# Four graph layers on one core: the search for other relations in the second stage instead of at the front, and a first stage without a branch

## The chip, the core and the metric

The kernel runs on one core of a Trainium2 chip. The metric is the device time of one execution in microseconds, lower is better. The kernel before takes 2770.98 us, the median of three runs (2770.6 to 2774.85). Of one more execution there is a profile.

## What is computed

128 graphs of 128 nodes with 128 features each pass through four layers; each is `x = x + layer(relu(layernorm(x)), adj)`. The adjacency `adj` is int32 and in this input holds only 0 and 1. Cut to what matters:

```python
# layer 0: relational graph layer, 8 relations
for r in range(1, 8):
    mask = (adj == r)
    agg += (mask / clip(mask.sum(2), 1e-6)) @ h @ rel_weights[r]
out = relu(layernorm(agg + h @ self_w.T + self_b) * gamma + beta)
# layer 1: attention from all pairs of nodes
D = abs(h[:, :, None, :] - h[:, None, :, :])
z = D @ W1.T + b1                        # 64 features per pair
z = batchnorm(z)                         # mean and variance over ALL pairs of ALL graphs
s = leaky(z) @ W2 + b2
A = softmax(where(adj > 0, s, -9e15))
y = leaky(batchnorm(A @ h @ Wg.T + bg))  # again over all graphs
out = concat(h, y) @ Wt.T + bt
# layers 2 and 3: graph attention with 4 heads and with 1 head, masked with adj > 0
```

Relations 2 to 7 matter in layer 0 alone. With an adjacency of 0 and 1 their sums are zero, and what remains of the sum over relations is relation 1.

## The kernel before

**Stages.** The batch norms cut the work into three stages. Line numbers are those of the kernel before.

- *First stage* (L265 to L781): layer 0 for groups of four graphs (32 groups, `chain`), and for each graph the differences of all pairs. Each graph has four *tiles* of differences, 512 in all. A tile goes through `difference` (L304: DVE, or POOL for tiles 1 and 3; L315), `absolute` (L362: ACT, not for tile 0, which is made with a maximum), `products` (L319: PE, L325 and L328, into PSUM `hp`), `evacuate` (L332: ACT, L339, PSUM to `z`) and `statistics` (L348: DVE). Two tiles of `z`, 1 MB, are stored to DRAM by SP (L346).
- *Second stage* (L830 to L1142): slots, one per graph. A slot takes two halves of `z` (loaded through a ring of ten buffers, L717), applies the batch norm (ACT, L908 and L912) and the leaky ReLU (DVE, L926), multiplies with W2 on PE (`ps`, L883) and turns the sums on PE (`pk`, L890). Every four slots the scores of a group go to DRAM and back (`rows`, L960 and L967), and a chain of attention steps follows, spread over later slots. `at(slot, place, work)` puts work at a place of a slot; "l" is after the scores of the slot before.
- *Third stage* (L1157 on): layers 2 and 3 in two versions, chosen with the flag `bounded` (L1099), that is, whether the attention scores are small enough to leave out the softmax's maximum. In this input the first version runs.

**Order of work.** The order inside the first stage is fixed when the program is built. `_ordered` (L118) takes steps with an engine, an estimated cost, the steps that they follow, and a rank; it walks through time and emits for each engine what could begin earliest. Each engine then runs its instructions in this order. The second stage is written out by slots. `with tc.manual_schedule()` keeps the order.

**Layer 0 in the front.** Relations other than 1 are treated apart:

- `part` (L573) loads all of `adj` in 16 parts of 512 KB as 128x1024 int32; `highest` (L577) takes the maximum of even parts on DVE (L583) and a sum of ReLU(adj - 1) of odd ones on ACT (L581); L587 to L597 make `flag` of these. All steps of group 0's layer 0 and a part of group 1's (the names in `FRONT`, L34) are ordered around this search in a first plan.
- `tc.If(flag)` (L653) runs the general sum over relations for all groups and writes it to DRAM as `AGG`; `cmp.Else()` (L700) writes the bias row `selfb` there for 31 groups (L702, 1792 and 6144 KB). This input takes the second way.
- A second plan (L779) holds the rest of the first stage. Each group from the second on loads its `agg` (L435) and adds it in `joined` (L492); group 0 adds `selfb` directly.

**The steps of a group that are named below**: `mask` (POOL, L452, adj == 1), `m8` (POOL, L530: adj > 0 as uint8, kept for all stages in `M8`), `deg` and `per` (DVE), `rs`, `rso`, `rsx` (POOL: reciprocal roots; `RS` is the last one), `hn` (ACT), `share` (POOL), `pt`, `pm`, `ph`, `po` (PE), `hT`, `maskT`, `hw` (ACT), `o` (DVE, L492), `on` and `end` (DVE), `h1` (ACT, L506), and in `features` `xp` (PE), `xe` (ACT), "again" (POOL, L410, a copy beside `xe` so that shifted reads wrap around), `pw` and `xw`.

**Users of `M8`**: `cap` in the second stage (POOL, L972: M8 * BIG + NEG12) and `off` in the third (POOL, L1202: M8 == 0).

Of the kernel before, what the change touches and what calls it, by code (L numbers as in the profile page):

```python
# [17 lines left out]
P = 128  # L18
G = 4
EPS = 1e-5  # L20
BIG = 3e38
# [11 lines left out]
AHEAD = 1  # L33
FRONT = {"load", "mask", "mv", "deg", "rs", "most", "per", "hn", "share", "pt", "hT", "pm", "maskT", "ph", "hw", "m8",  # L34
         "sd", "nb"}
PARTS, HELD = 16, 6
# [7 lines left out]
SEARCHED, BIAS = 5.5, 22.0  # L44
# [73 lines left out]
def _ordered(steps, limits, hop):  # L118
# [4 lines left out]
    free, done = dict.fromkeys(("SP", "Pool", "ACT", "DVE", "PE", "DMA"), 0.0), {}  # L123
# [16 lines left out]
    while len(plan) < len(steps):  # L140
# [17 lines left out]
        done[name] = start + cost + (0 if engine != "SP" else SEARCHED if name[0] == "part" else LANDING)  # L158
# [13 lines left out]
def tile_gnn_stack(ctx: ExitStack, tc: tile.TileContext, a: dict, out: bass.AP):  # L172
# [7 lines left out]
    early = ctx.enter_context(ExitStack())  # L180
    early_ring = ctx.enter_context(ExitStack())
    psum = early.enter_context(tc.tile_pool(name="psum", bufs=1, space=bass.MemoryType.PSUM))
    banks = {"sm": 2}
# [35 lines left out]
    slots = [dr.tile([G, P, ROW], F32, tag=f"rows{n}", name=f"rows{n}") for n in range(2)]  # L219
    M8 = [res.tile([P, G, P], U8, tag=f"m{g}", name=f"m{g}") for g in range(NG)]  # L220
# [42 lines left out]


    with tc.tile_pool(name="c0", bufs=1) as c0, tc.tile_pool(name="p0", bufs=2) as p0, ExitStack() as ctx0:  # L265

        both = c0.tile([P, 2, P], F32, name="both")
# [3 lines left out]
        sizes = (7, NG - 8)  # L271
        rest = [dr.tile([P, n, G, P], F32, tag=f"a{i}", name=f"a{i}") for i, n in enumerate(sizes)]
        AGG = [t[:, i, :, :] for t, n in zip(rest, sizes) for i in range(n)]
        AGG = [None] * AHEAD + AGG
        selfb = const.tile([P, G, P], F32, name="selfb")


        XP = [psum.tile([P, 4, P], F32, tag=f"xp{n}", name=f"xp{n}") for n in range(2)]
        gamma, beta = (t[:, 2, :] for t in XP)

        def shift(mv, rs):

            nb = small.tile([P, G], F32, name="lnnb")
            nc.gpsimd.tensor_tensor(nb, mv[:, :, 0], rs, OP.mult)
            nc.gpsimd.tensor_scalar(nb, nb, -1.0, None, op0=OP.mult)
            return nb
# [5 lines left out]
        H1 = {}  # L292
# [4 lines left out]
        steps = []  # L297

        def step(name, engine, cost, after, rank, work, takes=(), gives=()):
            steps.append((name, engine, cost, after, takes, gives, rank, work))  # L300

        XE, XW, diffs, linear, halves, stats = {}, {}, {}, {}, {}, {}

        def difference(i):  # L304

            b, t = divmod(i, NT)
            xe, k = XE[b // 2], b % 2
            on_pool = t in ON_POOL
            d = p0.tile([P, 2, KC, P], F32, tag=f"d{int(on_pool)}", name="d")
            x = xe[:, k, 0:P] if on_pool else XP[b // 2 % 2][:, k, :]  # L310
            ahead = xe[:, k, 1 + KC * t:]
            ahead = bass.AP(tensor=ahead.tensor, offset=ahead.offset,
                            ap=[list(ahead.ap[0]), [KH, 2], [1, KC], [1, P]])
            eng = nc.gpsimd if on_pool else nc.vector
            eng.tensor_tensor(d, ahead, x[:, None, None, :].to_broadcast([P, 2, KC, P]),  # L315
                              OP.max if t == BY_MAX else OP.subtract)
            diffs[i] = d.rearrange("p h k i -> p h (k i)")

        def products(i):  # L319
            d = diffs.pop(i)  # L320
            hp = linear[i] = big("hp").rearrange("p a b -> p (a b)")
            by_max = i % NT == BY_MAX
            for c in range(0, KC * P, 512):
                for hh in range(2):
                    nc.tensor.matmul(hp[64 * hh:64 * hh + 64, c:c + 512], w1T2 if by_max else w1T,  # L325
                                     d[:, hh, c:c + 512], start=True, stop=not by_max, skip_group_check=True)
                for hh in range(2 * by_max):
                    nc.tensor.matmul(hp[64 * hh:64 * hh + 64, c:c + 512], XW[i // NT // 2][:, i // NT % 2, :],  # L328
                                     both_t.rearrange("p h k i -> p h (k i)")[:, hh, c:c + 512],
                                     start=False, stop=True, skip_group_check=True)  # L330

        def evacuate(i):  # L332

            b, t = divmod(i, NT)
            if t % 2 == 0:
                halves[b, t // 2] = held_z()
            if t == 0 and b % G == 0:
                stats[b // G] = p0.tile([P, 2 * NT + 1, G, 6], F32, name="st")
            nc.scalar.copy(half_of(b, t), linear.pop(i))  # L339

        def half_of(b, t):
            return halves[b, t // 2][:, t % 2 * KC * P:(t % 2 + 1) * KC * P]

        def kept(b, half):
            to = HP[b][:, half * NT // 2:(half + 1) * NT // 2, :]
            nc.sync.dma_start(to.rearrange("p a b -> p (a b)"), halves[b, half])  # L346
# [1290 lines left out]
```

## Time and profile before

| what | value |
|---|---|
| median of 3 runs | 2770.98 us |
| profiled execution: time | 2768.47 us |
| profiled execution: span, first to last instruction | 2766.7 us |
| busy: PE, DVE, ACT, POOL | 2450.3, 2470.4, 2386.6, 1717.5 us |
| mean granted TensorE clock | 0.972 |
| DMA: moved, mean rate | 636.17 MB, 230 GB/s |
| flag made (DVE, L597) | 35.4 us |
| first difference (DVE, L315) | 43.0 us |
| first copy out of `hp` (ACT, L339) | 63.6 us |
| statistics of group 0 closed (L359) | 113.6 us |
| statistics of group 31 closed (L359) | 1520.8 us |
| first step of the third stage (POOL, L1202) | 2308.5 us |

All times inside the execution are counted from the start of the span. "Busy" is the time in which an engine works on an instruction; the idle time ahead of an instruction is put down to what released it, in brackets with an arrow. Releasers are inferred from semaphore events; "issue" is time in which an engine waited for nothing that the profile shows. A busy PE isn't PE at its peak, since its products are pipelined. "xN" is a number of like instructions. SP mainly issues DMAs.

### The profile page before, as it was taken

What the parts mean: (1) busy time and instruction counts of PE and PEld (TensorE: products, weight loads), DVE (VectorE), ACT (ScalarE), POOL (GpSimd) and SP (SyncE); (2) the same over time, 40 slices, a digit from 0 to 9 for tenths busy, and PEclk for the clock granted to TensorE, in tenths of its full rate; (3) what the DMA queues carried; (4) which work ended last, traced back from release to release, by engine and by line L of the source; (5) the groups of instructions that cost most, each with busy time, mean ns of one, the idle gap of its engine ahead of it and who ended that gap; (6) DMA issues with size and microseconds to landing.
All of it is one profiled execution on the core that took longest, in us unless ns stands there. A gap on an engine that the chain in (4) does not pass through costs nothing.

```text
span 2766.7 us, 42019 instructions
## 1 busy us (share of the span) xinstructions
PE 2450.3 (89%) x14521; PEld 1181.3 (43%) x14521; DVE 2470.4 (89%) x4712; ACT 2386.6 (86%) x2837; POOL 1717.5 (62%) x1629
## 2 busy tenths in 40 slices
PE   4899999999999999999998799988988887999886
PEld 2333333333333333333332344444444445777775
DVE  4999999999999999999999698888888887899986
ACT  4899999999999999999998787887878776898985
POOL 5899999999999999999987001100010115665642
PEclk7999999999999999999999899999999998999998
DMA  8455555555555555555543899999999971121110
GB/s 294 196 194 208 219 203 210 204 211 204 208 212 209 207 210 207 210 205 215 204 196 126 325 409 411 410 410 410 409 408 410 410 289 55 47 70 58 58 32 25
DMA packets 196203, 636.17 MB, mean 230 GB/s; under 512 B 32771, under 2 KB 100486, under 8 KB 132486
## 3 DMA queue, kind: packets, MB, share of 16 engines
q1 hardware_dynamic: 195536, 633.14, 59.9%
q8 instruction: 120, 1.97, 0.3%
q14 instruction: 109, 0.89, 0.1%
q10 hardware_dynamic: 438, 0.17, 0.0%
HBM read 329.10 MB, written 304.15 MB: 229 GB/s over the span
## 4 chain that ended last, share of the span: by engine, by line
ACT 34%; PE 22%; DVE 18%; issue 11%; DMA 10%; POOL 3%; SPq 0%; ACTq 0%; POOLq 0%; DVEq 0%
ACT d L363 12%; ACT z L339 11%; PE hp L325 6%; PE ps L883 5%; DMA rows<-sk 4%; DVE d L315 3%; DVE z L926 3%; DMA u<-rows 3%; DMA z<-hp 3%; PE hp L328 2%; ACT h L1241 2%; PE pk L890 2%; ACT hn L465 2%; ACT o L465 2%; ACT h L506 1%
## 5 line engine op out<-in xcount | busy, mean ns | idle before, releaser
L315 POOL TENSOR_TENSOR d<-xe 128x2048 f32<-128x2048 f32 x256 | 1074.2, 4202 | 59.7 <-PE hp L325 55.7
L325 PE MATMUL hp<-d,w1T 128*64 128x512 f32 x4096 | 998.6, 602 | 114.7 <-ACT z L339 99.1
L363 ACT ACTIVATE d<-d 128x2048 f32<-128x2048 f32 x384 | 734.7, 1935 | 14.7 <-POOL d L315 14.6
L315 DVE TENSOR_TENSOR d<-xe,xp 128x2048 f32<-128x2048 f32 x256 | 579.7, 2265 | 16.9 <-POOL xe L410 7.5
L325 PEld LDWEIGHTS hp<-d,w1T 128*64 128x64 f32 x4096 | 286.3, 137 | 635.6 <-issue 465.2
L339 ACT COPY z<-hp 128x1024 f32<-128x1024 f32 x512 | 516.3, 1028 | 44.6 <-PE hp L328 26.7
L974 POOL TENSOR_TENSOR x<-x,bt 128x512 f32<-128x512 f32 x32 | 48.5, 1517 | 674.1 <-DMA x<-x 544.4
L353 DVE BATCH_NORM_STATS2 st<-z 128x6 f32<-128x512 f32 x512 | 349.6, 683 | 53.7 <-ACT z L339 53.0
L354 DVE BATCH_NORM_STATS2 st<-z 128x6 f32<-128x512 f32 (+1 forms) x512 | 329.5, 643 | 0.0
L926 DVE SCALAR_TENSOR_TENSOR z<-z 128x2048 f32<-128x2048 f32 x128 | 293.2, 2291 | 4.0 <-ACT z L908 3.9
L908 ACT ACTIVATE z<-z,bias,scale 128x2048 f32<-128x2048 f32 x128 | 267.2, 2087 | 9.6 <-DVE bias L821 7.9
L912 ACT ACTIVATE zr<-z,bias,scale 128x2048 f32<-128x2048 f32 x128 | 267.3, 2088 | 0.9 <-PE ps L883 0.5
L328 PE MATMUL hp<-both_t,xw 128*64 128x512 f32 x1024 | 267.5, 594 | 0.0
L883 PE MATMUL ps<-z,w2z 128*32 128x512 f32 x1024 | 141.4, 624 | 61.9 <-DVE z L926 61.7
L890 PEld LDWEIGHTS pk<-pick,su 128*128 128x128 f32 x1024 | 127.8, 196 | 136.4 <-DVE su L904 98.8
L890 PE MATMUL pk<-pick,su 128*128 128x16 f32 x1024 | 140.2, 269 | 23.2 <-DVE su L904 22.6
L1357 PE MATMUL pv<-wr,e 128*128 128x128 f32 x1024 | 139.3, 281 | 5.9 <-DVE e L1334 4.0
L883 PE MATMUL ps<-zr,w2r 128*32 128x512 f32 x1024 | 142.5, 629 | 0.0
L328 PEld LDWEIGHTS hp<-both_t,xw 128*64 128x64 f32 x1024 | 80.7, 137 | 139.9 <-issue 139.9
L883 PE MATMUL ps<-z,w2l 128*32 128x512 f32 x1024 | 139.2, 612 | 0.0
L1357 PEld LDWEIGHTS pv<-wr,e 128*128 128x128 f32 x1024 | 126.7, 194 | 13.3 <-DVE e L1334 4.1
L1334 DVE SCALAR_TENSOR_TENSOR e<-e,ps 128x512 f32<-128x512 f32 x160 | 106.9, 677 | 26.2 <-ACT ps L1331 25.6
(243 smaller groups left out, 3823.1 us busy)
## 6 DMA issues: line engine op xcount, KB each, us to landing
hp<-z SPq DMA_DIRECT2D x248, 1024.0 KB, 4.1
z<-hp SPq DMA_DIRECT2D x248, 1024.0 KB, 14.2
x<-x SPq DMA_DIRECT2D x118, 256.0 KB, 6.0
u<-rows SPq DMA_DIRECT2D x32, 384.0 KB, 11.6
x<-in_x_dram SPq DMA_DIRECT2D x32, 256.0 KB, 5.6
adj<-in_adj_dram SPq DMA_DIRECT2D x32, 256.0 KB, 5.8
part<-in_adj_dram SPq DMA_DIRECT2D x16, 512.0 KB, 6.6
out_dram<-x SPq DMA_DIRECT2D x32, 256.0 KB, 2.4
```

What stands on the lines that cost most here:

```text
L315: eng.tensor_tensor(d, ahead, x[:, None, None, :].to_broadcast([P, 2, KC, P]), OP.max if t == BY_MAX else OP.subtract)
L325: nc.tensor.matmul(hp[64 * hh:64 * hh + 64, c:c + 512], w1T2 if by_max else w1T, d[:, hh, c:c + 512], start=True, stop=not by_max, skip_gr ...
L328: nc.tensor.matmul(hp[64 * hh:64 * hh + 64, c:c + 512], XW[i // NT // 2][:, i // NT % 2, :], both_t.rearrange("p h k i -> p h (k i)")[:, h ...
L339: nc.scalar.copy(half_of(b, t), linear.pop(i))
L353: nc.vector.bn_stats(st[:, 2 * t, :], hs[:, 0:512])
L354: nc.vector.bn_stats(st[:, 2 * t + 1, :], hs[:, 512:1024 - P * last])
L363: nc.scalar.activation(diffs[i], diffs[i], AF.Abs)
L883: nc.tensor.matmul(ps[32 * c:32 * c + 32, :], w[:, w0:w0 + 32], v[:, 512 * c:512 * c + 512], start=j0 == 0, stop=w is w2r, skip_group_chec ...
L890: nc.tensor.matmul(pk[:, kk, 0:16], su[:, kk, :], pick.rearrange("p h j -> p (h j)"), start=True, stop=True)
L908: nc.scalar.activation(z0, z0, AF.Identity, bias=bias1, scale=scale1[:, 0:1])
L912: nc.scalar.activation(zr, z1, AF.Relu, bias=bias1, scale=scale1[:, 0:1])
L926: nc.vector.scalar_tensor_tensor(z0, z0, 0.01, z0, op0=OP.mult, op1=OP.max)
```

## The change

- The two stages become one function `two_stages(general)`, called once with False ahead of the third stage, and a second time with True inside the last branch, where it does the first and second stage anew with the general sum, if the flag is set.
- With False there is no search, no `tc.If` and no `AGG` in the first stage: every group adds `selfb`. The first stage is a single plan; groups 1, 2 and 3 have all their steps in it, and begin `mask`, `mv` and `m8` after group 0's `rsx` or after certain products.
- `m8` keeps min(max(adj, 0), 2) instead of adj > 0 (two operations with numbers in the place of one comparison), so that `M8` tells other relations; its cost in the plan goes from 1.5 to 0.65. `BIG` is halved because `M8` may be 2.
- In the second stage `brief` gets 32 steps `highest` (two per slot from slot 21 on, DVE, one maximum over 128x512 uint8 of `M8` each), `highest_of_all`, a transpose on PE and `decided`, which makes `flag`, and `bounded` only if there are no other relations.
- The third stage's first version is unchanged. Its other branch stores the tiles kept on chip, runs `two_stages(True)` if the flag is set, and then the second version (moved into `last_stage`).
- Buffers that both calls use are made once through `fixed`.

The diff without changes of indentation, cut to its core:

```diff
-BIG = 3e38
+BIG = 1.5e38
+    def two_stages(general):
+        ahead_by = FETCHED - 2 * general
...
-        AGG = [None] * AHEAD + AGG
+    AGG = [dr.tile([P, G, P], F32, tag=f"a{g}", name=f"a{g}") for g in range(NG)]
...
-        def chain(g, agg=None, again=None):
+            def chain(g):
...
-            t = {}
+                t = {} if general else {"agg": selfb}
...
-            if agg is None:
+                if general:
                 step(("agg", g), "SP", 0.4, own("load"), s0 + 6, added)
-            else:
-                t["agg"] = agg
-            step(("mask", g), "Pool", 1.5, own("load"), s0 + 1, masked)
-            step(("mv", g), "DVE", 1.05, own("load"), s0 + 3, lambda: moments("x"))
+                begun = own("load") + ([("rsx", 0)] if g == 1 else [("hp", 12 * g - 22)] if g in (2, 3) else [])
+                step(("mask", g), "Pool", 1.5, begun, s0 + 1, masked)
+                step(("mv", g), "DVE", 1.05, begun, s0 + 3, lambda: moments("x"))
...
-            step(("m8", g), "Pool", 1.5, own("load"), s0 + 11,
-                 lambda: nc.gpsimd.tensor_scalar(M8[g], t["adj"], 0, None, op0=OP.is_gt))
+                step(("m8", g), "Pool", 0.65, begun, s0 + 11,
+                     lambda: nc.gpsimd.tensor_scalar(M8[g], t["adj"], 2, 0, op0=OP.min, op1=OP.max))
...
-        for c in range(PARTS):
-            step(("part", c), "SP", 21.3 / PARTS, [("top", c - HELD)], 1 + c / PARTS,
-                 lambda c=c: part(c))
-            step(("top", c), "ACT" if c % 2 else "DVE", 1.35, [("part", c)], -6, lambda c=c: highest(c))
-        step("top", "DVE", 0.4, [("top", c) for c in range(PARTS)], -99, highest_of_all)
-        step("ptop", "PE", 0.3, ["top"], -99, one_row, takes=("sm",))
-        step("flag", "DVE", 0.4, ["ptop"], -99, flagged, gives=("sm",))
...
-        with tc.manual_schedule():
-            for work in _ordered(steps, {"sm": 2}, HOP1):
-                work()
-        steps.clear()
-        ctx0.close()
...
-        with tc.If(nc.values_load(flag, min_val=0, max_val=1) > 0) as cmp, \
-                tc.tile_pool(name="cr", bufs=1) as cr, tc.tile_pool(name="pr", bufs=1) as pr:
+            def relations():
+                with tc.tile_pool(name="cr", bufs=1) as cr, tc.tile_pool(name="pr", bufs=1) as pr:
...
+            if general:
...
+                relations()
-        with cmp.Else():
-            for t, n in zip(rest, sizes):
-                nc.sync.dma_start(t.rearrange("p n g t -> p n (g t)"),
-                                  selfb.rearrange("p g t -> p (g t)")[:, None, :].to_broadcast([P, n, G * P]))
...
-        step("bias", "DMA", BIAS, [], -99, lambda: None)
...
-            if g > 3:
                 chain(g)
...
+                def highest(g):
+                    nc.vector.tensor_reduce(t["tops"][:, g:g + 1], M8[g].rearrange("p a b -> p (a b)"), AX.X, OP.max)
+
+                def highest_of_all():
+                    nc.vector.tensor_reduce(t["tops"][:, NG:NG + 1], t["tops"][:, 0:NG], AX.X, OP.max)
+
+                def one_row():
+                    t["pm"] = sm("pm")
+                    nc.tensor.transpose(t["pm"][0:1, 0, :], t["tops"][:, NG:NG + 1], ident)
+
+                def decided():
+                    above, bound = (t["tops"][0:1, NG + n:NG + n + 1] for n in (1, 2))
+                    nc.vector.tensor_reduce(above, t["pm"][0:1, 0, :], AX.X, OP.max)
+                    nc.vector.tensor_scalar(above, above, 1.5, None, op0=OP.is_gt)
+                    nc.vector.tensor_copy(flag, above)
+                    nc.vector.tensor_scalar(bound, t["bound"][0:1, :], 4.0, None, op0=OP.is_gt)
+                    nc.vector.tensor_tensor(above, above, bound, OP.max)
+                    nc.vector.tensor_scalar(bounded, above, 0.5, None, op0=OP.is_lt)
...
+                for g in range(NG):
+                    at(end + 9 + g // 2, "l", lambda g=g: highest(g))
+                at(searched, "l", highest_of_all)
+                at(searched + 1, "p", one_row)
+                at(searched + 1, "l", decided)
...
+    two_stages(False)
...
+    with cmp.Else():
+        for g in Y:
+            nc.sync.dma_start(Z[g], Y[g])
+            nc.sync.dma_start(X[g], X1[g])
...
+        with tc.If(nc.values_load(flag, min_val=0, max_val=1) > 0):
+            two_stages(True)
+        last_stage()
```

## The prediction

> **What bounds the kernel now.** I read, in this order, the table of busy time by stretch, the timeline of the first 110 us, the chain of waits of the front and of one steady stretch, and the groups and waits of the second stage.
>
> The table by stretch has, after the stretch, the busy time of PE, PE's weight loads, DVE, ACT and POOL, then the granted clock, the DMA share and the rate.
>
> ```profile
> 30.00:40.00 10.00, 0.37 (x1) 0.08 (x1) 4.75 (x15) 3.77 (x8) 3.20 (x5) 0.50 0.76 241
> 50.00:60.00 10.00, 3.06 (x16) 0.75 (x12) 2.29 (x1) 1.67 (x1) 8.75 (x5) 0.82 1.04 393
> 600.00:800.00 200.00, 187.03 (x904) 73.04 (x902) 193.48 (x338) 190.24 (x207) 189.47 (x114) 1.00 0.57 211
> 1600.00:1800.00 200.00, 180.29 (x1357) 86.88 (x1353) 172.67 (x287) 162.62 (x116) 19.06 (x16) 0.97 1.03 410
> ```
>
> From 200 to 1400 us (first stage) four engines are 93 to 97% busy: only the start can give much. From 1550 to 2210 (second stage) the DMA engines are full and DVE is 86% busy. The front is half idle; its timeline shows two holes:
>
> ```profile
> 33.87 1.65 ACT L506 ACTIVATE h<-x,lnnb,RS 128x128 f32<-128x128 f32 x4 [0.47 <-POOL lnnb L285]
> 35.37 0.14 DVE L597 TENSOR_SCALAR flag<-top 1x1 int32<-1x1 f32 x1
> 39.72 1.34 SPq L702 DMA_DIRECT2D a<-selfb  x2
> 41.58 0.66 PE L393 MATMUL xp<-ident,h 128*128 128x128 f32 x2 [6.56 <-DVEq L653]
> 42.71 0.29 POOL L410 COPY xe<-xe 128x128 f32<-128x128 f32 x1 [5.64 <-ACT xe L397]
> 63.63 1.01 ACT L339 COPY z<-hp 128x1024 f32<-128x1024 f32 x1 [11.96 <-issue]
> ```
>
> The flag is there at 35.51, the first product after the branch starts at 41.58: 6.1 us. Then ACT stands still for 11.96 us ahead of its first copy out of PSUM. The chain from 30 to 70 us names the cause:
>
> ```profile
> 40.51 11.16 DMA a<-selfb
> 51.67 11.73 issue
> 63.63 1.02 ACT z L339
> ```
>
> The copy waits on a DMA semaphore; the write of 7936 KB of `a` (L702) runs until about 62.6, so I take it for that write. DVE, PE and POOL stand still with it for 11.6 to 12.3 us.
>
> In the steady part the order of instructions repeats with each group of four batches; equal PE rows of the chain lie 45.62 us apart (999.03 and 1044.66). No piece of that chain from 1000 to 1092 is POOL's: it runs ACT, PE, ACT, DVE, ACT. POOL's waits from 200 to 1400 us, and ACT's on it:
>
> ```profile
> POOL d L315 <- PE hp L325: 25.5, 68, 1.5
> ACT d L363 <- POOL d L315: 11.0, 23, 1.1
> ```
>
> **What the Trainium skill says.** (1) "GPSIMD Engine Reference", section Performance versus the Vector engine: bodies of one or two operations run at 1.03 cycles per element, data-dependent branching costs some 12 cycles per element. My estimate from this for 512 elements at the stated 1.2 GHz is 0.44 us and dispatch. The trace has 0.62 us for multiply and add on `M8` (L972) but 1.50 us for comparisons (L530, L452): it agrees for arithmetic; no page prices comparisons or min and max. (2) "VectorE: DVE Perf Modes", The perf-mode tier table: `tensor_reduce` has only the 1x mode; at the stated 0.96 GHz 512 elements are 0.53 us. The trace has 0.676 us (L988, f32). (3) "DMA: Bandwidth & Descriptors", Specifications: 435 GB/s is the ceiling of 16 engines; the second stage holds 410. (4) "Runtime: NRT & Kernel Launch", Instruction fetch mechanics: a taken branch out of the fetched window stalls on a fetch; the 6.1 us here agree in direction.
>
> **The change part by part.** The sum is made against the profiled execution: 2768.47 us, of which 2766.7 are span. The median of the runs shown, 2770.98, lies 2.5 us higher.
>
> 1. *Search out of the front.* It takes away 16 reads of 512 KB, 8 reductions on DVE (1.20 us each) and 8 passes on ACT (1.15 + 0.19). I follow group 0 to the copy `xe` on POOL ("again"), which releases the first differences. Before, ACT's search, the next group's `hn` and late `hw` (18.45) put the last product of `po` at 22.7. Without them, with the same durations: `hn` 8.28 to 9.93, PE's transposes and the three broadcasts until 12.04 as before, `pm` to 13.1, `ph` 1.92 to 15.0, `hw` 0.6 to 15.65, `po` 3.6 to 19.3. The mask's share is done by 11.0 even with `m8` at 1.50 and hides behind the broadcasts. From `po` to the end of `RS` it took 33.84 - 22.7 = 11.1 with DVE free when needed: 30.45. That is 3.4 us.
> 2. *Branch out.* Before, "again" came 8.9 us after `RS`. In the new order POOL has mask 1 (1.50), `m8` 1, the roots of group 1 (1.95) and one small step (0.23) ahead of it, with gaps 4.35 us if `m8` takes 0.65, 5.2 if 1.5; `h`, `xp` and `xe` (1.65 + 0.4 + 0.4) hide behind that. "Again" starts at 34.8 instead of 42.71: 7.9 us for parts 1 and 2 together.
> 3. *`AGG` out.* No write of 7936 KB, no 31 loads of 256 KB; the joining step reads `selfb`. In the built order the first copy of z has no DMA wait left: -11.96. What is late next is that copy's PE product and ACT's queue, costed in 4. The 31 loads lie in a stage whose DMA share is 0.57; I cost them at nothing. Without that cover each would cost its landing, 4.8 us.
> 4. *Group 1's front moves into the pipeline.* From the first abs to the 16th copy ACT has 50.3 us of work instead of 48.9, to the 128th 385.6 instead of 384.4 (counts of the built orders times the durations above). PE gets `pm`, `ph` and `po` of group 1, 5.2 us in a stretch where it has slack of some tenth. I take +2; ends 0 and +6.
> 5. *Steady period.* From the seventh group on, PE, DVE, ACT and POOL have in both programs the same repeated sequence, apart from the new `m8`. The table is no proof that `m8` gains 0.85 us (the plan's cost is no measurement): between 0.62 (L972) and 1.50 (L530); I take 0.65. As POOL isn't in the chain, 0. A gain is possible: ACT waits 0.39 us per period for the POOL difference behind `m8`, 25 periods make 10 us at most; but right after it ACT waits 0.94 us for PE anyway. A loss is excluded: the same sequence with a shorter step.
> 6. *Other transients.* Before, groups 1 to 7 took 322.4 us (113.55 to 435.94) instead of 7 x 45.62 = 319.3: 3.1 us. The new plan has fewer odd groups; I take the same, ends -3 and +4.
> 7. *Maximum in the second stage.* 32 reductions of 128x512 uint8, two per slot (a slot scores one batch) from slot 21 to 36, at 0.68 us (f32, L988; the bytes could make it 0.53 to 1.2, the page's 1x and the search's 128x1024): 21.8 us on DVE, and six tiny steps and a transpose, about 1.3. Behind them on DVE's queue are the copy `su` and the leaky ReLU on z, for which PE's `pk` and `ps` wait. The cover is DMA:
>
> ```profile
> z<-hp SPq DMA_DIRECT2D x203, 1024.0 KB, 14.2
> L988 DVE TENSOR_REDUCE mx<-e 128x4 f32<-128x512 f32 x26 | 17.6, 676 | 0.0
> L926 DVE SCALAR_TENSOR_TENSOR z<-z 128x2048 f32<-128x2048 f32 x111 | 253.9, 2288 | 2.1 <-ACT z L908 2.1
> ```
>
>    Four slots take 23.6 us on average (all bytes at 410 GB/s), but 22.3 where no DMA ends the wait. DVE is busy 20.3 of them, and 5.4 more make 25.7: it falls 2.1 us behind the DMA per four slots, 8.5 us in all. Loads are issued 14.2 us ahead of landing, so the queue doesn't run dry; later the compute makes up 1.3 us per four slots for 22 of these, 28 us. So 0, and +1.5 for a short dry spell; ends 0 and +9; with no cover at all +23.
> 8. *Third stage.* Same operations on `M8`; the branch reads a flag made long before: 0. `BIG`, `fixed` and the code in the other branch do nothing on this data.
>
> Sum: -7.9 - 12.0 + 2 + 0 + 0 + 1.5 = -16.4. On the profiled time 2752.1; on the median 2754.6, which I give as 2754.5.
>
> **The rivals.**
> - *The forecast*: 2754.5, from its own ends 2748 to 2761. Chance 0.56.
> - *POOL's slack shortens the period.* For: POOL is 95% busy and ACT does wait for it. Against: the chain. 0.39 to 0.6 us on 25 periods, 10 to 15 us: 2742. Chance 0.14.
> - *Part of the reductions shows, or the new start has worse transients.* For: between 1590 and 1766 the chain has DVE and PE and hardly a DMA, and a clock dip (PE's products 1.5 times as long about 1715) needs the same reserve. Against: loads keep their 14 us through it. 8 to 10 us: 2763. Chance 0.18.
> - *`m8` isn't faster* (the change doesn't do what it says): the front loses 0.85, the period nothing: 2755.4; within the forecast.
> - *Slower: the reductions lie wholly in the open.* Place: DVE ahead of `su` and the leaky ReLU in slots 21 to 36. Price: 23 us at 0.68, 33 at 1.0. It decides once a reduction takes over about 0.9 us and the queue runs dry, so that DMA, full afterwards, never makes it up: 32 x 0.95 + 1.3 = 31.7 instead of 1.5, 2785. Chance 0.06. The remaining 0.06 lies between, about 2770.
>
> **How the numbers follow.** This kernel's measurement tells 0.2%, 5.5 us, from no change. Below 2765.4: the forecast, the period's rival and two thirds of the third: 0.83. Within: 0.11. Above 2776.5: 0.06. The range goes from the period's rival to the bulk of the third: 2742 to 2766.
>
> **What would show it.** Right: no work of L583 or L702, first difference at 34 to 36 us, no gap over 3 us before the first z; equal PE rows 45.62 us apart; `m8` at about 0.65; second stage still at 410 GB/s and as long as before. Wrong: a period other than 45.62 (part 5), a first stage that ends less than 12 us earlier (parts 1 to 4), or DMA under 400 GB/s in the stretch of the reductions (part 7).

## The result and the profile after

| | before | after |
|---|---|---|
| median of 6 runs | 2771.51 us (2767.95 to 2778.03) | 2754.82 us (2750.12 to 2760.07) |
| ratio after/before, 95% interval | | 0.9938 [0.9922, 0.9953] |
| profiled execution, its span | 2768.47, 2766.7 us | 2756.67, 2754.8 us |
| copy "again" of the first pair starts | 42.71 us | 34.08 us |
| first copy of z out of PSUM starts | 63.63 us | 44.95 us |
| last aggregate of group 0 starts | 113.55 us | 92.39 us |
| last aggregate of the first stage starts | 1520.81 us | 1497.79 us |
| from there to the last leaky ReLU of the second stage | 747.7 us | 752.8 us |
| from there to the last DVE instruction | 494.2 us | 499.0 us |

The changed kernel is 0.6% faster, 16.7 us by the medians. The stages show that this is not one gain of 16.7: the first stage ends 23.0 us earlier, the second gives 5.1 back, and the third, whose code and order are the same, took 4.9 longer in this execution (14 profiled kernels with that third stage lie between 493.4 and 500.1 us, so I read nothing into it). With it the profiled execution gained 11.8 us, not 16.7.

The table by stretch of the kernel after, in the stretches of the prediction (after the stretch: PE, PE's weight loads, DVE, ACT, POOL, granted clock, DMA share, GB/s):

```profile
30.00:40.00 10.00, 8.27 (x24) 4.24 (x26) 5.35 (x4) 5.95 (x14) 9.44 (x11) 0.50 0.05 17
50.00:60.00 10.00, 8.42 (x42) 2.61 (x38) 9.96 (x23) 9.54 (x10) 9.43 (x10) 1.00 0.45 184
600.00:800.00 200.00, 185.70 (x887) 71.34 (x888) 194.14 (x333) 189.80 (x207) 185.28 (x112) 1.00 0.54 205
1600.00:1800.00 200.00, 170.39 (x1278) 81.42 (x1266) 184.19 (x305) 151.32 (x106) 19.51 (x16) 0.97 1.02 397
```

The stretch from 50 to 60 us, which had PE at 3.06 and DVE at 2.29 busy, is now nearly full. From 30 to 40 us PE is busy 8.27 us instead of 0.37, but at half clock (0.50); part 4 of the last account comes back to that. The steady part is as it was, with POOL at 185.3 instead of 189.5. From 1600 to 1800 DVE has 11.5 us more work, and the DMA rate is 397 instead of 410 GB/s: that is where time came back.

The timeline of the front after, ACT's and POOL's lines around the two old holes:

```profile
29.66 1.65 ACT L503 ACTIVATE h<-x,lnnb,RS 128x128 f32<-128x128 f32 x4 [5.43 <-POOL lnnb L287]
31.06 0.61 POOL L526 TENSOR_SCALAR m<-adj 128x512 uint8<-128x512 int32 x1
34.08 0.29 POOL L412 COPY xe<-xe 128x128 f32<-128x128 f32 x1
44.95 1.01 ACT L341 COPY z<-hp 128x1024 f32<-128x1024 f32 x1
```

`h` starts at 29.66 (before 33.87), `m8` takes 0.61 us, "again" stands 4.4 us behind `h` (before 8.8), and the first copy of z follows 10.9 us after "again" (before 20.9), with no wait noted.

### The profile page after: what moved, and what is told of

It is laid out like the page before. It is cut to its first block, busy times and chain, and to the rows that moved or that the text cites. A ratio compares the mean times of both kernels' runs of the same rounds, so it can differ in the third digit from the quotient of the medians.

```text
span 2754.8 us, 41902 instructions
## 1 busy us (share of the span) xinstructions
PE 2450.1 (89%) x14521; PEld 1183.4 (43%) x14521; DVE 2477.0 (90%) x4738; ACT 2378.7 (86%) x2821; POOL 1699.9 (62%) x1628
## 4 chain that ended last, share of the span: by engine, by line
ACT 34%; PE 22%; DVE 19%; issue 11%; DMA 8%; POOL 5%; SPq 0%; ACTq 0%; POOLq 0%; DVEq 0%
ACT d L365 11%; ACT z L341 11%; PE ps L814 5%; PE hp L327 5%; DVE z L857 4%; DVE d L317 3%; DMA z<-hp 3%; DMA rows<-sk 3%; PE hp L330 2%; POOL d L317 2%; PE pk L821 2%; DMA u<-rows 2%; ACT h L1392 2%; ACT o L462 2%; ACT h L503 2%
## 5 line engine op out<-in xcount | busy, mean ns | idle before, releaser
L857 DVE SCALAR_TENSOR_TENSOR z<-z 128x2048 f32<-128x2048 f32 x128 | 299.4, 2339 | 7.9 <-ACT z L839 7.9
L839 ACT ACTIVATE z<-z,bias,scale 128x2048 f32<-128x2048 f32 x128 | 267.1, 2087 | 10.1 <-DVE bias L751 7.9
## 6 DMA issues: line engine op xcount, KB each, us to landing
u<-rows SPq DMA_DIRECT2D x32, 384.0 KB, 11.6
```

The lines of the kernel that those rows point to most:

```text
L857: nc.vector.scalar_tensor_tensor(z0, z0, 0.01, z0, op0=OP.mult, op1=OP.max)
```

## The experiments

All were run beside the kernel before; a ratio is against its runs. "Last aggregate" is the last one of the first stage. The first stage of the changed kernel was run unchanged in five kernels; its last aggregate fell at 1495.8 to 1497.8 us, so a difference under 2 us there says nothing. "The second stage" is the time from there to the last leaky ReLU. In the eight profiled kernels without reductions in it, the kernel before among them, it took 747.0 to 750.0 us, so 3 us between two of them say nothing either. With two reductions in a slot it took 752.8 us in the changed kernel and 754.7 in the one with `m8` as a comparison (below), whose second stage is the same.

### What the reductions in the second stage cost

**Search left out of the changed kernel.**

```
 def highest(g):
-    nc.vector.tensor_reduce(t["tops"][:, g:g + 1], M8[g].rearrange("p a b -> p (a b)"), AX.X, OP.max)
+    if g == 0:
+        nc.vector.memset(t["tops"][:, 0:NG], 0.0)
```

> The changed kernel without its 32 reductions over M8 in the second stage (one memset of their results stands in; the search for other relations is left out). The stretch from the last aggregate of the first stage to the last leaky ReLU of the second took 747.7 us in the kernel before and 752.8 in the changed one. Theory (the reductions on DVE make the slots slower than the DMA, the loads of z lose their reserve, and DMA time is lost for good): 747 to 748 us, no stretch of 20 us from 1640 to 1800 below 400 GB/s, and the total 5 us less than the changed kernel's, about 2750. Rival (a clock dip near 1745 us and not the reductions emptied the queue): 752 to 753 again, and a stretch at 360 to 375 GB/s stays.

Measured: 2751.34 us, ratio 0.9925 [0.9912, 0.9939]; the second stage took 750.0 us. From the table by stretch, first of the changed kernel:

```profile
1680.00:1700.00 20.00, 15.69 (x120) 7.21 (x119) 18.64 (x29) 13.16 (x12) 1.88 (x2) 1.00 1.02 397
1700.00:1720.00 20.00, 16.98 (x126) 8.80 (x130) 18.61 (x32) 16.41 (x12) 1.89 (x2) 0.95 1.00 380
1720.00:1740.00 20.00, 17.91 (x135) 7.71 (x132) 18.12 (x35) 16.02 (x11) 0.96 (x1) 0.97 1.00 359
1740.00:1760.00 20.00, 18.85 (x128) 9.65 (x128) 17.83 (x29) 12.65 (x10) 0.92 (x2) 0.83 0.99 374
```

and of the one without the search:

```profile
1680.00:1700.00 20.00, 15.68 (x128) 7.46 (x120) 16.26 (x27) 16.63 (x12) 3.81 (x2) 1.00 1.03 409
1700.00:1720.00 20.00, 17.92 (x114) 8.15 (x114) 15.82 (x26) 10.88 (x9) 2.46 (x2) 0.83 1.02 408
1720.00:1740.00 20.00, 18.46 (x147) 9.35 (x143) 17.34 (x32) 15.74 (x11) 2.19 (x2) 1.00 1.03 413
1740.00:1760.00 20.00, 18.05 (x143) 8.35 (x140) 17.43 (x29) 18.40 (x13) 1.20 (x1) 1.00 1.03 409
```

With the search the four rates fall short of 410 by 13, 30, 51 and 36 GB/s; times 20 us that is 2.6 MB, which take 6.3 us at 410 GB/s. Without it no stretch is short, though the clock dips there too (0.83). So the reductions emptied the queue, not the clock. The stage took 750.0 us, between the theory (747 to 748) and the rival (752 to 753). The 2.3 us above the kernel before arise after slot 115 by the times of the leaky ReLU. The kernel before without its search, whose second stage has no reductions either, ends 1.8 us later than the kernel before in the same slots, so I take these 2.3 us for scatter.

**One reduction in a slot instead of two.**

```
-searched = end + 9 + NG // 2
+searched = end + 9 + NG
...
-    at(end + 9 + g // 2, "l", lambda g=g: highest(g))
+    at(end + 9 + g, "l", lambda g=g: highest(g))
```

> The changed kernel with one reduction in each of 32 slots in place of two in each of 16. Four slots take 23.6 us at the DMA's rate. If DVE's busy time counts (20.3 us per four slots and 2.7 of reductions make 23.0), the reserve of the loads holds: 747 to 749 us from the last aggregate of the first stage to the last leaky ReLU, total about 2750. If the chain through DVE, PE and ACT counts (22.3 and 2.7 make 25.0), each four slots fall 1.4 us behind, 11 us over eight of them, as much as in the changed kernel: 752 to 754 us, total about 2755.

Measured: 2752.12 us, ratio 0.9924 [0.9908, 0.9939]; the second stage took 747.9 us, as before the change, with all stretches of 20 us from 1640 to 1800 at 408 to 414 GB/s. The same 21.8 us of reductions cost nothing that shows when spread. By the chain the slots would have fallen 11 us behind; by the times of the leaky ReLU they were at most 2.2 us behind the kernel before. DVE's busy time decides here (23.0 against 23.6 us), not the chain.

**Each reduction twice.**

```
 def highest(g):
-    nc.vector.tensor_reduce(t["tops"][:, g:g + 1], M8[g].rearrange("p a b -> p (a b)"), AX.X, OP.max)
+    for _ in range(2):
+        nc.vector.tensor_reduce(t["tops"][:, g:g + 1], M8[g].rearrange("p a b -> p (a b)"), AX.X, OP.max)
```

> The changed kernel with each of the 32 reductions done twice, so four in each of 16 slots. Theory: with the queue dry each us of DVE shows. Four slots take 20.3 + 10.9 = 31.2 us by DVE's busy time, or 22.3 + 10.9 = 33.2 by the chain, against 23.6 by DMA: 30 to 38 us behind after 16 slots, less a reserve of about 5. The second stage from the last aggregate of the first to its last leaky ReLU takes 772 to 785 us instead of 752.8, total 2775 to 2787. Rival (the reductions are hidden and something else cost the 5 us): below 758 us, total below 2760.

Measured: 2779.26 us, ratio 1.0026 [1.0020, 1.0033]; the second stage took 779.1 us. Table by stretch:

```profile
1680.00:1700.00 20.00, 14.56 (x114) 7.26 (x118) 18.54 (x31) 12.93 (x10) 3.16 (x1) 1.00 0.87 322
1700.00:1720.00 20.00, 12.74 (x94) 5.99 (x85) 19.66 (x32) 11.48 (x8) 0.62 (x1) 0.91 0.82 288
```

21.8 us more on DVE made the stage 26.3 longer than in the changed kernel. Once the loads' reserve is used up, every further us shows. The stage is 31.4 us longer than before the change, near the 31.7 that the slower case of the prediction had put there for 30 us of reductions; it took 43.8 us of them.

**The search by OR on words.**

```
 def highest(g):
-    nc.vector.tensor_reduce(t["tops"][:, g:g + 1], M8[g].rearrange("p a b -> p (a b)"), AX.X, OP.max)
+    words = M8[g].rearrange("p a b -> p (a b)").bitcast(I32)
+    most = t["wt0"].bitcast(I32)
+    nc.vector.tensor_tensor(most, words if g == 0 else most, words, OP.bitwise_or)
...
-    nc.vector.tensor_reduce(t["tops"][:, NG:NG + 1], t["tops"][:, 0:NG], AX.X, OP.max)
+    nc.vector.tensor_reduce(t["tops"][:, NG:NG + 1], t["wt0"].bitcast(U8), AX.X, OP.max)
```

> The changed kernel with the search done by OR: in the same slots and places one bitwise OR of 128 words (the 512 bytes of M8 read as int32) into a running tile, in place of a reduction of 512 bytes; then one reduction of the 512 bytes of that tile. The OR should take 0.28 us (a tensor_tensor of 64 to 256 elements takes 0.28 to 0.42 us) instead of 0.676: 9 us on DVE instead of 21.8. Theory: four slots then take 22.5 us by DVE's busy time or 24.5 by the chain, at most 0.9 behind per four, 3.5 us in all, within the reserve: 747 to 749 us for the second stage, total 2749 to 2751. Rival (any work on DVE ahead of su and the leaky ReLU shows by its length): 40% of 5.1 us remain, 749.7, total 2752.

Measured: 2749.35 us, ratio 0.9918 [0.9905, 0.9932]; the second stage took 748.3 us. The operations on that tile (duration min/median/max in ns, first and last start):

```profile
L1036 DVE TENSOR_TENSOR selfb<-selfb,m x31: 260/291/893, 1627.4 to 1721.3; 128x128 int32<-128x128 int32 x31
L1039 DVE TENSOR_REDUCE selfb<-selfb x1: 681/681/681, 1726.5 to 1726.5; 128x1 f32<-128x512 uint8 x1
```

0.29 us instead of 0.68 for the same bytes. This kernel still does the whole search, and is 5.5 us under the changed kernel by the medians; the intervals of the two ratios overlap. The stage's length is the better sign: 748.3 us, and 746.8 in the last kernel below, which has the OR too, both as without reductions. Theory and rival lie only 1 to 3 us apart here, too near for this run to tell one from the other.

### What the parts of the front were worth

Six kernels start from the kernel before and leave parts out; each result is read at the marks of this table. "write" says whether the 7936 KB of `a` are written.

| kernel | write | h | again | first z | again to first z | first z to group 0's aggregate | last aggregate |
|---|---|---|---|---|---|---|---|
| before | yes | 33.87 | 42.71 | 63.63 | 20.9 | 49.9 | 1520.8 |
| no search | yes | 33.4 | 38.00 | 57.11 | 19.1 | 49.0 | 1514.1 |
| no search, POOL's order kept | yes | 32.08 | 36.71 | 55.82 | 19.1 | 50.0 | 1504.5 |
| no write of a | no | 34.0 | 43.15 | 51.78 | 8.6 | 45.7 | 1503.8 |
| neither | no | 34.13 | 38.45 | 47.59 | 9.1 | 45.3 | 1498.0 |
| neither, no branch | no | 36.18 | 38.14 | 46.73 | 8.6 | 45.7 | 1499.8 |
| neither, no branch, POOL's order kept | no | 31.92 | 33.88 | 44.46 | 10.6 | 45.4 | 1493.5 |
| after | no | 29.66 | 34.08 | 44.95 | 10.9 | 47.4 | 1497.8 |

**The write alone.**

```
-with cmp.Else():
-    for t, n in zip(rest, sizes):
-        nc.sync.dma_start(t.rearrange("p n g t -> p n (g t)"),
-                          selfb.rearrange("p g t -> p (g t)")[:, None, :].to_broadcast([P, n, G * P]))
...
-    chain(g)
+    chain(g, selfb)
```

> The kernel before with its search and its branch, but without the write of a in the else branch and without the loads of a; all groups add selfb directly (the relations' sums, which this data does not need, are left out of the result). Theory (the write alone holds the first copy of z, 11.96 us): first copy at 51.7 us instead of 63.6, last aggregate of the first stage at 1509 instead of 1520.8, total 2759. Rival (the copy's product or ACT's queue is late next, or the loads of a cost or cover something): first copy at 55 or later, or a last aggregate more than 2 us from 1509.

Measured: 2754.21 us, ratio 0.9943 [0.9926, 0.9959]. In total this is as fast as the whole change, with the search and the branch still at the front: its first stage ends 6.0 us later than the changed kernel's, but its second stage gives nothing back (748.1 us), and its third took 4.0 us less, which is within that stage's scatter. The first copy came at 51.78, as forecast to 0.1 us; the last aggregate came 17.0 earlier, not 12. Group 0 shows most of the rest: from the first copy to its aggregate 45.65 us instead of 49.92. The timeline of PE after the standstill, kernel before:

```profile
64.70 7.17 PE L325 MATMUL hp<-d,w1T 128*64 128x512 f32 x20 [11.63 <-ACT z L339]
```

and without the write:

```profile
51.38 3.60 PE L325 MATMUL hp<-d,w1T 128*64 128x512 f32 x16
55.64 1.94 PE L325 MATMUL hp<-d,w1T 128*64 128x512 f32 x8 [0.65 <-ACT z L339]
```

A product took 7.17 / 20 = 359 ns there and 3.60 / 16 = 225 here. The table by stretch of the kernel before gives the cause in the third value from the end, the granted clock:

```profile
60.00:65.00 5.00, 0.30 (x2) 0.29 (x4) 0.33 (x1) 1.37 (x2) 0.00 (x0) 0.50 0.47 178
65.00:70.00 5.00, 5.00 (x14) 1.29 (x12) 4.62 (x13) 3.37 (x3) 0.00 (x0) 0.50 0.38 157
70.00:75.00 5.00, 5.00 (x26) 1.65 (x24) 5.00 (x8) 3.94 (x3) 3.82 (x1) 0.99 0.57 210
```

After 11.6 us without work PE comes back at half clock, at 64.70 us, and has it whole again at 70.1 us, 5.4 us later. The Trainium skill, "TensorE: Matmul & The Clock Gate", Part 1, says this: PE falls to half clock after an idle window of about 3.4 us and needs at least one such window of sustained work to come back. The trace agrees: PE stands still from 53.1 us, the granted clock falls at 56.4, and the way back took longer than one window. 20 products x 134 ns are 2.7 of the 4.3 us; the other 1.6 us I did not trace.

**The search alone.** Where search is left out, the flag is set to 0 by a memset and the 16 parts and their reductions are gone.

```
-for c in range(PARTS):
-    step(("part", c), "SP", ...
-    step(("top", c), "ACT" if c % 2 else "DVE", ...
...
+step("flag", "DVE", 0.1, [], -99, lambda: nc.vector.memset(flag, 0))
```

> The kernel before without its search (no reads of adj in 16 parts, no reductions, the flag is set to 0 by one memset), with branch and write of a kept. First theory (the branch holds every engine until the front is done, so the write starts as late against the front as before): roots done at 29.6 to 30.5 us instead of 33.84, copy again at 38.5 to 39.4, first copy of z 3.4 to 4.3 us earlier than before, 59.3 to 60.2, last aggregate at 1516.5 to 1517.4, total 2766. Second theory (with the flag known at the start SP passes the branch alone and the write starts as soon as selfb is there, beside the front): first copy of z at 47 to 50, last aggregate at 1503 to 1507, total 2755.

Measured: 2764.94 us, ratio 0.9975 [0.9966, 0.9984]. Neither theory came true. "Again" came at 38.0, near the first theory's 38.5 to 39.4, but not for the reason given: `h` hardly moved. The first copy (57.1) and the last aggregate (1514.1) came 2 us before that theory's range, and far behind the second's. In the built order, with the parts gone, an `m8` stood in the midst of group 0's roots on POOL, waiting for its load until 9.7 us. (It was group 2's; the expectation of the run with the order held calls it group 1's.)

**Neither search nor write; and without the branch too.**

```
-with tc.If(nc.values_load(flag, min_val=0, max_val=1) > 0) as cmp, \
-        tc.tile_pool(name="cr", bufs=1) as cr, tc.tile_pool(name="pr", bufs=1) as pr:
-    ...
```

> The kernel before without its search and without write and loads of a; the branch stays, on a flag set to 0 by a memset (search and relations left out). By the sum: search 3.4 to 4.3 us and write 12.0, so again at 38.5 to 39.4, first copy of z at 47.4 to 48.2, last aggregate at 1504.5 to 1505.5, total 2755. Rival (with the flag known at the start the branch costs next to nothing, since its 6 us were the wait for the flag and the way from it to the engines): again at 34 to 35, last aggregate at 1500 to 1501, total 2750.

> As the kernel before without search, write and loads of a, and without the branch too; the first stage remains in its two plans, with group 1's front in the first one, and m8 stays a comparison (search and relations left out). By the sum the branch is worth 4.5 us and one plan instead of two costs 2: again at 34 to 35, first copy of z at 43 to 44, last aggregate at 1496 to 1498 less 2 against the changed kernel's 1495.8 to 1497.8, so 1494 to 1496, total 2747. Rival (one plan is no loss but a gain, which explains why the changed kernel's first stage ends 5 us earlier than the sum): last aggregate at 1499 to 1503, total 2752 to 2755.

Measured: 2749.97 us, ratio 0.9921 [0.9905, 0.9938] with the branch, and 2752.96 us, ratio 0.9934 [0.9917, 0.9951] without it. Timeline with the branch:

```profile
34.13 1.65 ACT L506 ACTIVATE h<-x,lnnb,RS 128x128 f32<-128x128 f32 x4 [5.50 <-POOL lnnb L285]
37.29 0.69 PE L393 MATMUL xp<-ident,h 128*128 128x128 f32 x2 [11.86 <-ACTq L647]
38.45 0.29 POOL L410 COPY xe<-xe 128x128 f32<-128x128 f32 x1 [4.36 <-ACT xe L397]
```

and without it:

```profile
36.18 1.65 ACT L506 ACTIVATE h<-x,lnnb,RS 128x128 f32<-128x128 f32 x4 [5.49 <-POOL lnnb L285]
36.72 0.86 PE L393 MATMUL xp<-ident,h 128*128 128x128 f32 x2 [8.96 <-ACT h L506]
38.14 0.29 POOL L410 COPY xe<-xe 128x128 f32<-128x128 f32 x1 [2.00 <-ACT xe L397]
```

With the branch "again" (38.45) and the first copy (47.59) came where the sum put them. For "again" that is luck: `h` is as late as before (34.13), and the branch took 4.5 us less instead. The last aggregate, at 1498.0, came 6.5 us before its place: 4.7 of these are there at group 0's aggregate, since the slow restart after the write is gone as well, and 2.1 arise in later groups. Without the branch "again" was expected at 34 to 35 and came at 38.14. With the branch PE waits for ACT's sequencer at the branch (ACTq L647), 3.16 us after `h` starts; without it PE follows the first quarter of `h` by 0.54. So in this pair a branch whose flag is long known costs 2.6 us at PE and 2.4 at "again" (4.32 against 1.96 us after `h`); what the sequencers do in that time the profile does not show. In the kernel before "again" was 8.84 behind `h`: another 4.5 us were the wait for the late flag. By its numbers the rival held here (last aggregate 1499.8, total 2753.0). But `h` itself came 2 us later, which used up the gain, and another 2.0 us went between the aggregates of groups 0 and 7. The late `h` is an order of POOL's again, with group 2's `m8` first of all and group 0's mask behind it, at 11.59 instead of 4.68.

**The same with POOL's order held.** So I planned group 1's mask and all `m8` behind `share`.

```
-step(("mask", g), "Pool", 1.5, own("load"), s0 + 1, masked)
+step(("mask", g), "Pool", 1.5, own("load") + [("share", 0)] * (g == 1), s0 + 1, masked)
...
-step(("m8", g), "Pool", 1.5, own("load"), s0 + 11,
+step(("m8", g), "Pool", 1.5, own("load", "share"), s0 + 11,
```

> As the kernel before without its search (left out; the flag is 0), but group 1's mask and both m8 are planned behind group 0's share, since in the earlier run without the search the planner had put m8 of group 1 ahead of group 0's roots on POOL, where it waited for its load and cost 4.6 us. Theory (without the search the roots of group 0 are done at 29.6 to 30.5 us instead of 33.84): again follows 5.2 us later, 34.8 to 35.7, first copy of z 19.1 after that, 53.9 to 54.8, last aggregate at 1510.9 to 1511.8 instead of 1520.8. Rival (the search did not hold the roots): again at 38 and last aggregate at 1514, as in the earlier run.

Measured: 2756.86 us, ratio 0.9946 [0.9931, 0.9961]. "Again" at 36.71 lies between the theories; `h` came 1.8 us earlier than before, not 3.4 to 4.2. The timeline names what else held group 0:

```profile
11.93 1.65 ACT L465 ACTIVATE hn<-x,lnnb,lnrs 128x128 f32<-128x128 f32 x4 [1.89 <-POOL lnnb L285]
15.89 3.25 PE L483 MATMUL ph<-both,hT 128*128 128x128 f32 x16
18.98 0.39 PE L488 MATMUL po<-both,hT 128*128 128x128 f32 x2
```

This `hn` is group 1's, eight of the 16 products of `ph` are group 1's, and group 0's `po` stands behind them at 18.98; in the kernel after it starts at 14.63. In the kernel before it was no later:

```profile
19.08 0.80 PE L488 MATMUL po<-both,hT 128*128 128x128 f32 x2 [0.15 <-ACT hw L478]
19.67 0.63 PE L489 MATMUL po<-hw,maskT 128*128 128x128 f32 x2
```

So with group 1's steps in place, taking the search away moved the start of `po` by 0.1 us. The other 1.7 us of `h` come from the speed of `po`'s products, 0.39 instead of 0.63 us for two of them; both speeds also occur in one and the same code (see the end). The later marks of this kernel can't be used: its repeated sequence differs from the one before, and it gained another 8.6 us after group 0's aggregate. In that sequence five groups take 227.0 us, 45.40 each instead of 45.62, so the period of the kernel before is no floor; which step of the order makes the difference stays open.

The same edit of POOL's order, with write and branch left out as well:

> As the kernel before without search, write and loads of a, and branch (relations left out), in its two plans, with the same edit of POOL's order. Theory: roots done at 29.6 to 30.5, again 2.6 us later, 32.2 to 33.1, last aggregate at 1494 to 1495, total 2747; the changed kernel's one plan (1495.8 to 1497.8) then costs the 2 us of part 4. Rival (one plan is a gain): again at 34 or later, last aggregate at 1498 or later.

Measured: 2745.20 us, ratio 0.9902 [0.9887, 0.9917], "again" at 33.88, 0.8 us behind the theory, since `h` started at 31.92 only; last aggregate at 1493.5, 0.5 us before it. It leaves the other relations out and has no search, so it is no rival to the changed kernel. Of its lead of 4.3 us at the last aggregate, 2.1 arise after group 7, in a steady sequence that differs here too. What it tells apart is the start: from the first copy of z to group 0's aggregate the two plans take 45.3 to 45.7 us in all four kernels without the write, the one plan 47.4. That fits the 2 us of part 4 in size; which of the moved steps costs them was not tested.

### The period, and the way to "again"

**m8 as a comparison.**

```
-lambda: nc.gpsimd.tensor_scalar(M8[g], t["adj"], 2, 0, op0=OP.min, op1=OP.max))
+lambda: nc.gpsimd.tensor_scalar(M8[g], t["adj"], 0, None, op0=OP.is_gt))
```

> The changed kernel with m8 as the comparison of before (1.50 us) in place of min and max (0.61), planned at the same 0.65, so the order is the same (values above 1 are then not told apart in M8, so other relations would not be found). Theory (POOL is not in the steady chain): 45.62 us a group, 1084.8 from the aggregate of group 7 to that of group 31, the first stage at most 2 us later, total 2755 to 2757. Rival (POOL at 95% busy sets the period): 46.0 to 46.5 a group, the first stage 10 to 21 us later, total 2765 or more.

Measured: 2759.03 us, ratio 0.9951 [0.9935, 0.9967]. 45.62 us a group up to the last three, 1084.9 us from group 7's aggregate to group 31's in this kernel, in the changed one and in the kernel before. The last aggregate came at 1499.7, 1.9 to 3.8 us later than in the five runs of the faster `m8`, all of it by group 7's aggregate. The total lies 2 us above the theory's 2755 to 2757 and far below the rival's 2765. ACT's waits from 600 to 800 us in the changed kernel:

```profile
ACT z L341 <- PE hp L330: 6.0, 5, 1.2
ACT xw L407 <- DVE d L317: 3.5, 4, 0.9
```

and with the comparison:

```profile
ACT z L341 <- PE hp L330: 3.8, 4, 1.0
ACT xw L407 <- DVE d L317: 3.6, 4, 0.9
ACT d L365 <- POOL d L317: 1.9, 5, 0.4
```

A slower `m8` makes ACT wait 1.9 us for POOL and 2.2 less for PE right after.

**Group 1 behind "again".** The changed kernel with the OR, and

```
-begun = own("load") + ([("rsx", 0)] if g == 1 else [("hp", 12 * g - 22)] if g in (2, 3) else [])
+begun = own("load") + ([("again", 0)] if g == 1 else [("hp", 12 * g - 22)] if g in (2, 3) else [])
```

> The changed kernel with the OR search, and with group 1's mask, m8 and roots planned behind the first copy again on POOL instead of behind the roots of group 0. In the changed kernel POOL does 4.35 us of group 1 between the roots and again, while h, xp and xe need only 2.5. Theory: again about 2 us earlier (31 us), last aggregate of the first stage 2 us less than in the run with the OR search alone, 1493.8, total 2747. Rival (group 1's front then comes late, and the start is ended by its chain and not by the first difference): group 0 ends earlier, but the last aggregate stays at 1495.8 or later, total 2749 or more.

Measured: 2748.66 us, ratio 0.9923 [0.9909, 0.9936]. "Again" came at 30.35, 2.4 us earlier than with the OR alone, but the first copy at 42.92 (42.97) and the last aggregate at 1496.4 (1495.8): no gain. The rival held; the chain of this kernel:

```profile
40.00 0.60 PE pt L472 x4
...
40.63 0.60 ACT hT L475
41.22 1.81 ACT d L365
...
43.08 1.96 PE hp L327 x8
```

Group 1's transpose and `hT` have moved into the way of the first copies.

## Why the prediction was right, part by part

The total was met (2754.5 against 2754.82) by two errors of opposite sign: the first stage gained 23.0 us instead of 17.9, and the second gave back 5.1 in the profiled execution instead of 1.5. That the difference is 0.3 us is luck. (One sum of the chances is off by a hundredth: 0.56, 0.14 and two thirds of 0.18 are 0.82, not 0.83.) The signs and the two holes were right; in part 1 the cause was split wrongly, and the terms for the write, for group 1's front and for the reductions were too small.

The 23.0 us, read at the marks of both kernels: 4.2 up to `h`, 4.4 from `h` to "again", 10.1 from "again" to the first copy of z, 2.5 from there to group 0's aggregate, 1.8 up to group 7's, nothing after.

1. *Search out of the front* (3.4 us at the roots). In the kernel after `h` starts 4.2 us earlier. But the search alone, with POOL's order held, moved the start of group 0's `po` by 0.1 us (19.08 to 18.98), and without write and branch too it started at 18.83. It came at 14.63 only when group 1's front had left the first plan as well. I had named group 1's `hn` in the queue, but put the gain down to the search, and counted group 1's move in part 4 only, as a cost. What group 1's move alone is worth, with the search in place, was not run. The 4.2 compares two executions with slow products in `po`; with the fast ones of the OR kernel `h` starts at 28.36 us.
2. *Branch out* (4.5). From `h` to "again" 8.84 became 4.42: 4.4. Right in sum. It is made of 4.5 for a flag that comes late, 2.4 for the branch itself, and 2.5 given back by group 1's work on POOL. Taking those 2.5 away gains nothing, since PE and ACT then do group 1 later.
3. *Write of a out* (12.0). The mis-sized term of the first stage: taken out alone it is 11.85 at the first copy, as priced, but 16 to 17 at the aggregates. A wait of 11.6 us on PE costs its length and then slow products; the half clock from 60 to 70 us was there to be read in the table by stretch of the kernel before.
4. *Group 1's front into the pipeline* (+2). +1.9 from the first copy to group 0's aggregate (47.4 against 45.3 to 45.7 in the two-plan kernels without the write), as priced. But from "again" to the first copy the changed kernel takes 10.9 us, where the kernel without the write takes 8.6. ACT does steps of group 1 just ahead of that copy, and waits for PE before each:

```profile
43.56 0.60 ACT L475 ACTIVATE maskT<-pt 128x512 f32<-128x512 f32 x1 [1.18 <-PE pt L472]
44.45 0.60 ACT L475 ACTIVATE hw<-ph 128x512 f32<-128x512 f32 x1 [0.30 <-PE ph L480]
```

   PE comes late to them, and this front runs at half clock (0.50 from 30 to 40 us, whole from 41.9 on). The chain of the kernel after has, just ahead:

```profile
36.74 1.98 PE hp L327 x4
38.72 1.71 PE hp L330 x4
40.43 1.65 PE hp L327 x4
42.08 0.86 PE hp L330 x4
```

   At the speed of the last row the first three would take 2.6 us instead of 5.3. I estimate from this that ACT's waits of 1.5 us would go at full clock; no run shows it. The clock of the front is in no part of the prediction.
5. *Steady period* (0). Right: 45.62 us in both, and again with a slow `m8`. The rival that POOL's slack shortens the period falls; the 0.89 us saved only become idle time on POOL. `m8` took 0.612 us against 0.65 taken.
6. *Other transients* (0, ends -3 and +4). From group 0's to group 7's aggregate 320.5 us instead of 322.4: -1.8. Within the ends.
7. *Reductions in the second stage* (+1.5, ends 0 and +9). The other mis-sized term: +5.1 in the profile, and 3 to 5 us when taken away, spread or shortened (medians 2751.3, 2752.1, 2749.4 against 2754.8). Each took 0.676 us as forecast, and the slots fell behind by 9.1 us between slot 20 and slot 40, against 8.5 forecast. The sign of being wrong that was named for this part, DMA under 400 GB/s, came true. What failed is "Loads are issued 14.2 us ahead of landing, so the queue doesn't run dry". The landing times of z in the changed kernel, one line each for 1640 to 1660, 1700 to 1720, 1740 to 1760 and 1880 to 1900 us (DMA issues; count, size, median us from issue to landing):

```profile
z<-hp SPq DMA_DIRECT2D x6, 1024.0 KB, 10.4
...
z<-hp SPq DMA_DIRECT2D x6, 1024.0 KB, 8.3
...
z<-hp SPq DMA_DIRECT2D x6, 1024.0 KB, 7.6
...
z<-hp SPq DMA_DIRECT2D x6, 1024.0 KB, 14.1
```

   At 10.4 us the rate is still 410 GB/s, at 8.3 it is 380. So a landing time of some 10 us goes with the full rate, and what was in reserve is only the part above it: 3 to 4 us by these figures, not 14. I take the 10 us for the load's own way beside its like, which no run shows apart. The chain of waits of that stretch shows the DVE lag turn into waits for a load that was issued only when a late pass of ACT had read its buffer:

```profile
1686.97 1.76 ACT zr L843
1688.73 6.50 DMA z<-hp
...
1714.45 6.54 DMA z<-hp
```

   Some 6 of the 9 us behind were lost DMA time, as computed from the rates above, which agrees with the 5.1 within the stage's scatter; the later slots made up the rest.
8. *Third stage* (0). Same code, 499.0 against 494.2 us in these two executions, 493.4 to 500.1 over 14 kernels: no effect that can be told from its own scatter.

## What to carry to other kernels

Here work put on a busy engine under a full DMA was free only up to the difference of the two rates: compare DVE's busy time for a few slots, new work included, with the DMA's time for the same slots (for four slots 25.7 against 23.6 us cost 3 to 5 us, 23.0 cost nothing), and spread the work until it fits. Don't count the time from issue to landing as reserve; look for the landing time at which the rate begins to fall. Price a standstill of PE at its length plus the products that follow at half clock, and look at the granted clock of a front before costing its products. When a planner orders the instructions, compare its new order on every engine, and the durations of like instructions, before putting a difference down to what was removed.

## What the runs showed of the hardware

- After a standstill of 11.6 us PE had half clock for another 5.4 us of work: 359 ns instead of 225 a product.
- In one pair of kernels a branch on a flag that had long been known cost 2.4 to 2.6 us between ACT, PE and POOL; on a flag just written, it took 6.1 us from the flag to the first product.
- On POOL min and max on 128x512 int32 to uint8 take 0.61 us, a comparison of the same size 1.50.
- On DVE a bitwise OR of 128 words took 0.29 us, a maximum over the same 512 bytes 0.68.
- The front's products ran at two speeds from one execution to the next: 0.63 us for two of `po` until 17.8 us in the changed kernel, 0.39 from 15.7 us with the OR, in the same code. The granted clock of the two traces is on record only from 18.0 and 15.3 us on, whole at first, so a half clock ahead of that is likely but not shown. The speed makes 1.3 of the 2 us by which the first stage's end varied.
